# Query and key transposes one unit earlier, and the first causal mask ahead of the first expert piece, in a kernel that weaves attention into two mixtures of experts

## Chip, cores and metric

The kernel runs on one core of a Trainium2 chip. The metric is the device time of one execution in microseconds, as the median of several executions. Inputs and outputs are fp32 and lie in HBM.

## What is computed

The input x has 8 sequences of 512 tokens of 128 numbers. The reference applies three residual steps: half of a mixture-of-experts layer, causal attention, and half of the same mixture again, each on a layer norm of x.

```python
x = x + 0.5 * ffn(layernorm(x))
x = x + attn(layernorm(x))
x = x + 0.5 * ffn(layernorm(x))
```

The mixture has 8 experts (128 to 512 to 128, relu between). A router picks the two best experts of each token, and their outputs are added with softmax gates. The attention has 16 heads of 8 numbers. On half of the heads the queries and keys are rotated by position, on half a linear decay with the distance is added to the scores; all are causal. The softmax divides by the sum of the exponentials.

## The kernel before, in words

**Stages.** The first mixture takes its tokens in three groups (f0, f1, f2), the second in three (g0, g1, g2). For each group tokens are routed, scattered by expert to HBM, read back per expert, run through the expert, and their results gathered and added. The attention takes (sequence, head group of four heads, step) as one unit: 8 x 4 x 3 = 96 units, numbered 0 to 95, twelve to a sequence, three to a head group. Units below 0 and above 95 hold expert work alone. Everything is woven together in one program: while attention runs for one sequence, experts of the first mixture work for later sequences and experts of the second mixture for earlier ones.

**Order.** The order of instructions on TensorE (PE), ScalarE (ACT), VectorE (DVE) and SyncE (SP) is the order in which the program is written out; no scheduler moves them. Each engine goes through its own stream in turn, and instructions on different engines wait for each other where data or buffers require it.

**A unit** is written by `surround` (L1458). It issues, in this order:

- `scores` (L1222): score matmuls of four heads into `st` (one buffer of four PSUM banks), written transposed with keys on the partitions; then two exponentials on ScalarE (L1238), each of two heads, into `ee`. Step 0 has one key tile of 512 queries, step 1 one of 384, step 2 two of 256 and 128.
- `values` (L1251) of the unit before: matmuls of `ee` with the values into `o`; after a head group's last step ScalarE copies `o` to `oT`.
- one piece of expert work (`fill`). A piece is a transposition of gathered rows (`turn`, L996, tile xbT, copied to xT), one of four matmuls of the first layer (`wide`, L1010, tile z, relu to h), or one tile of the second layer (`out`, L1034, tile y, bias added on VectorE to ysb). `m.evac` says which engine evicts turn and wide here: VectorE in attention units, but ScalarE in units 8, 9 and 10 of a sequence.
- `causal` (L1241) for the first two heads: VectorE takes the minimum of the exponentials and a mask (L1245). Its instruction becomes the *mark*; evictions of wide and out become the mark too. An indirect DMA on POOL (scatter, send, gather) is made to wait for the last mark, which keeps these transfers apart.
- `m.transfer`: one such indirect DMA.
- `outputs` (L1268) of the head group that ended: transposes, a reciprocal and a multiplication on VectorE.
- `causal` for the other two heads.
- the work due in this unit, each stream a step at a time, with expert pieces spread between (the rest of the unit's quota, some two pieces a unit in all); then additions and a second transfer.

**Due work.** `at(u, stream, steps)` (L1431) files the steps of a stream under units u, u+1 and so on; streams filed first are taken first within a unit. For sequence b with first unit u = 12 b:

- `project` (L1157) in the eight units from u - 10 to u - 3: layer norm, transposition, the matmuls for queries, keys and values (L1169), rotation (L1186 to L1192), and as the last step VectorE writes the scaled queries into `qpad` (L1195) and the keys into `kpad` (L1198). There is one qpad and one kpad; each head has 32 columns in them.
- `operands` (L1201) for head group g, two steps: four TensorE transposes of qpad (L1208) and a VectorE copy to `qT` (L1214), then the same for kpad with a ScalarE copy to `kT`. qT and kT have two buffers each.
- `finish` (output projection of the attention) and `route` (router of the second mixture; its steps on VectorE L838 to L937).

During attention three PSUM banks serve all else (pool m: pieces, transposes, projections, router), one serves `o` and four serve `st`.

Of the kernel before, what the change touches and what calls it, by code (L numbers as in the profile page):

```python
# [1333 lines left out]
def macaron_kernel(  # L1334
# [24 lines left out]
    def run(*streams):  # L1359
        for s in streams:  # L1360
            for _ in s:
                pass
# [12 lines left out]
    def take(stream, n):  # L1375

        for _ in range(n):
            if next(stream, STOP) is STOP:
                return
            yield  # L1380
# [5 lines left out]
    with ExitStack() as main:  # L1386
        m = Main(tc, main, aps)
# [17 lines left out]
        def close(g):  # L1405
            m.close_group(g, order.index(g))

        def opened(g):

            pieces = m.experts(g)  # L1410
            next(pieces)
            return pieces

        def step(*streams):
            for st in streams:
                next(st, None)

        def transfers(n):
            for _ in range(n):
                m.transfer()  # L1420
# [4 lines left out]
        units = [(b, g, s) for b in range(B) for g in range(G) for s in range(len(m.STEPS))]  # L1425
        per = len(m.STEPS)
# [4 lines left out]
        def at(u, stream, steps, each=1):  # L1431

            for k in range(steps):
                due.setdefault(u + k // each, []).append((stream, 1))

        def routed(u, shares, urgent=False, ahead=False):
            early = u < 0 or u > core
            r = m.route(shares, urgent, ahead, early)
            steps = 7 if early else 8
            if u > core:  # L1440
                at(u, r, 3 + steps, 3)
                return
            if shares[0][0] is not f1:
                at(u, r, 3)
                u += 3
            at(u, r, steps)

        def combined(u, g, i, dst=None, urgent=False, ahead=False):
            at(u, m.combine(g, i, dst, urgent, ahead), 1)
# [8 lines left out]
        def surround(n, att):  # L1458

            m.unit = n  # L1460
            now = None
            for g, fetch, start, end in plan:
                if n == fetch:
                    close(g)
                    fills[g.key] = [opened(g), g.pieces]
                if n == end:
                    run(fills[g.key][0])
                if start <= n < end:
                    now, until = fills[g.key], end
                    if g is g1 and att:  # L1470
                        until = end + 7
            quota = min(now[1], -(-now[1] // (until - n))) if now else 0
            fill = now[0] if now else iter(())
            if now:
                now[1] -= quota
            if att:
                ee = m.scores(*units[n])
            last, m.oT = m.oT, None
            if m.held is not None:
                got = m.values(*m.held)  # L1480
                if got is not None:
                    m.oT = (*m.held[:2], got)
            m.held = (*units[n], ee) if att else None
            m.evac = "dve" if att and n % seq not in (8, 9, 10) else "act"
            run(take(fill, 1 if quota else 0))
            m.evac = "act"
            if att:
                m.causal(units[n][2], ee, 0)
            m.transfer()
            if last is not None:  # L1490
                m.outputs(*last)
            if att:
                m.causal(units[n][2], ee, 1)
            if not att:
                m.additions()
            work = due.pop(n, [])
            todo = max(quota - 1, 0)
            for k, (stream, steps) in enumerate(work):
                some = todo // (len(work) - k + 1)
                run(take(stream, steps))  # L1500
                run(take(fill, some))
                todo -= some
            if n >= core and len(m.jobs) + len(m.results) > 2:
                run(take(fill, todo // 2))
                todo -= todo // 2
                m.transfer(second=True)
            run(take(fill, todo))
            m.additions()
            m.transfer(second=True)

        m.held = m.oT = None
        with m.banks(("m", 8)):

            n = [m.normalise(b) for b in range(5)]
            r = [m.route([(f0, 0)], early=True), m.route([(f0, 1)], early=True),
                 m.route([(f1, 0)], True, early=True)]
            step(n[0], n[0], n[1], n[1], n[0], n[0])
            step(r[0], n[1], n[1], r[0], r[1], r[0], r[0])
            transfers(8)
            step(r[1], r[1], r[1], n[2], n[2])  # L1520
            transfers(8)
            step(n[3], n[3], n[4], n[4], *[r[0], r[1]] * 3, n[2], n[2])
            step(r[2], r[2], r[2], n[3], n[4], n[3], n[4])
            run(*r[:2], *n)
            m.bias_columns()

            at(first, r[2], 4)
            routed(first + 1, [(f1, 1)], urgent=True)
            routed(first + 3, [(f1, 2)], urgent=True)
            routed(-22, [(f2, 0)], urgent=True)  # L1530
            combined(-16, f0, 0, urgent=True, ahead=True)
            routed(-14, [(f2, 1)], urgent=True)
            combined(-12, f0, 1, urgent=True)
            routed(-10, [(f2, 2)], urgent=True)
            at(-10, m.project(0), 8)
            for b in range(B):
                u = b * seq
                if b == 2:
                    combined(7, f1, 0, urgent=True, ahead=True)
                elif b > 2:  # L1540
                    combined(u - (17 if b == 5 else 21), *place[True][b][0], urgent=b == 5, ahead=b == 5)
                if b > 0:
                    at(u - 10, m.project(b), 8)
                for g in range(G):
                    at(u + g * per - 2, m.operands(b, g), 2)
                at(u + seq + 2, m.finish(b), 2, 2 if b == B - 1 else 1)
                routed(u + seq + (3 if b == B - 1 else 4), place[False][b], urgent=b in (1, 4, 5, 6, 7), ahead=b in (4, 6, 7))
            for i in range(2):
                combined(79 + 7 * i, g0, i, out)
            for i, (_, t0, t1) in enumerate(g1.shares):  # L1550
                at(tail + 2 + 3 * i, m.collect(g1, i, out), 1 + t1 - t0)
            at(tail, m.verdict(bad), 2)

            for u in range(first, 0):
                surround(u, False)
                if u == first:
                    m.attention_constants()
                for _ in range(min(2, len(m.loads))):
                    m.loads.popleft()()
        with m.banks(("st", 1), ("o", 1), ("m", 3)):  # L1560
            for u in range(core + 2):
                surround(u, u < core)
                if u >= 12 and m.later:
                    m.later.popleft()()
        with m.banks(("m", 8)):
            for u in range(core + 2, ends):
                surround(u, False)
            run(fills["g2"][0])
            assert not due, due
            assert not m.jobs and not m.adds  # L1570
            while m.results:
                m.transfer()
            last = [m.collect(g2, i, out, parts=min(2, g2.shares[i][2] - g2.shares[i][1])) for i in range(4)]
            step(*last)
            run(*last)
# [53 lines left out]
```

## Time and profile before

| | us |
|---|---|
| median of 9 runs | 695.67 (694.57 to 698.71) |
| the profiled execution | 696.78 |
| its span | 695.1 |
| TensorE matmuls busy | 623.6 |
| VectorE busy | 405.9 |
| ScalarE busy | 343.9 |
| POOL busy | 295.8 |
| first and last score matmul (start) | 145.9 and 562.0 |
| query copies to qT, 32 | 21.8 |
| key copies to kT, 32 | 18.8 |
| masks, 192 | 93.3 |

A profile is of one execution, so what is worked out from it is set against that execution's own time, 1.1 us above the median. PEld is the weight load of TensorE, which runs beside matmuls. Matmuls are pipelined and their ends are modelled, so that the start of the next one tells more than the end of the last. A line of the timeline gives start and length in us, engine, line of the kernel, operation, tiles out and in, shapes and a count; in brackets stands how long the engine sat idle before it and what ended that.

### The profile page before, as it was taken

To read this page: it belongs to the slowest core of one execution; us is meant where nothing else is said; L and a number is where in the kernel's file an instruction comes from. 1 tells how busy PE (TensorE), PEld (TensorE's weight loads), DVE (VectorE), ACT (ScalarE), POOL (GpSimd) and SP (SyncE) were. 2 spreads that over 40 slices of the span, in tenths; PEclk is the share of its full clock that TensorE was granted. 3 is DMA by queue.
4 is the path that set the end of the run, shared out by engine and by line. 5 is a ranking of instruction groups with operands and counts; after the bars stand their busy time and mean duration, and the time that the engine had idled before them with its cause. 6 is when DMAs were issued, how large, how long until landed. Compare 5 with 4: busy or idle time off the path is not lost. (4 is left out here: it accounts for less than half of the span.)

```text
span 695.1 us, 12906 instructions
## 1 busy us (share of the span) xinstructions
PE 623.6 (90%) x4797; PEld 403.5 (58%) x4797; DVE 405.9 (58%) x1432; ACT 343.9 (49%) x552; POOL 295.8 (43%) x318
## 2 busy tenths in 40 slices
PE   3269989999999999999999999989999998979980
PEld 2148867756556656555656566545556566747760
DVE  6736437735457575675676687777666654333424
ACT  4034434455665656566566566566645542234420
POOL 3745627653132314414144425333244556665550
PEclk9999999999999999999999999999999998999995
DMA  8747843222409951011211111112212121145224
GB/s 264 197 136 204 213 111 100 71 63 71 106 24 143 199 193 38 24 27 42 71 29 43 49 33 37 31 31 71 60 30 63 32 58 42 39 137 150 82 66 153
DMA packets 80229, 61.32 MB, mean 88 GB/s; under 512 B 7400, under 2 KB 73888, under 8 KB 80160
## 3 DMA queue, kind: packets, MB, share of 16 engines
q1 hardware_dynamic: 71296, 42.79, 24.2%
q0 software_dynamic: 8576, 17.63, 8.5%
q8 instruction: 40, 0.66, 0.4%
q14 instruction: 29, 0.24, 0.1%
q10 hardware_dynamic: 288, 0.01, 0.0%
HBM read 26.21 MB, written 34.19 MB: 87 GB/s over the span
## 5 line engine op out<-in xcount | busy, mean ns | idle before, releaser
L1238 ACT ACTIVATE ee<-st 128x768 f32<-128x768 f32 (+1 forms) x192 | 159.2, 882 | 90.4 <-PE st L1231 85.1
L479 POOL DMA_INDIRECT yt_f<-ys,back_f x64 | 65.3, 1020 | 130.8 <-DVE ee L1245 55.9
L1245 DVE TENSOR_TENSOR ee<-ee,keep 128x256 f32<-128x256 f32 (+1 forms) x192 | 93.3, 507 | 22.2 <-ACT ee L1238 21.9
L1037 PEld LDWEIGHTS y_f<-w_sb,h_f 128*120 128x120 f32 (+1 forms) x704 | 85.9, 182 | 28.5 <-issue 16.2
L1231 PE MATMUL st<-qT,kT 32*128 32x512 f32 (+3 forms) x1024 | 96.1, 467 | 5.7 <-ACT kT L1214 3.3
L1037 PEld LDWEIGHTS y_g<-w_sb,h_g 128*128 128x128 f32 x640 | 81.3, 193 | 32.2 <-issue 25.5
L895 POOL DMA_INDIRECT xs<-xn_g,to_g x64 | 63.9, 999 | 84.7 <-DVE ee L1245 32.5
L1037 PE MATMUL y_f<-w_sb,h_f 128*120 128x128 f32 (+1 forms) x704 | 93.9, 277 | 0.2 <-DVE h_f L1022 0.2
L1013 PE MATMUL z_f<-xT_f,w_sb 128*128 128x480 f32 (+1 forms) x192 | 90.8, 562 | 1.0 <-ACT xT_f L1004 1.0
L1013 PE MATMUL z_g<-xT_g,w_sb 128*128 128x512 f32 (+1 forms) x192 | 89.7, 554 | 1.4 <-ACT xT_g L1004 0.7
L1257 PE MATMUL o<-ee,vpad 128*32 128x512 f32 (+3 forms) x1024 | 89.6, 442 | 0.8 <-DVE ee L1245 0.8
L1020 ACT ACTIVATE h_f<-z_f,b1T 128x480 f32<-128x480 f32 (+1 forms) x86 | 53.6, 625 | 70.1 <-PE z_f L1013 69.4
L1037 PE MATMUL y_g<-w_sb,h_g 128*128 128x128 f32 x640 | 85.9, 279 | 0.5 <-DVE o_tok L1280 0.3
L981 POOL DMA_INDIRECT ys<-ysb_g,home_g x64 | 62.9, 983 | 51.2 <-ACT h_g L1020 16.7
L1020 ACT ACTIVATE h_g<-z_g,b1T 128x512 f32<-128x512 f32 (+1 forms) x77 | 49.5, 645 | 54.1 <-PE z_g L1013 53.8
L1041 DVE TENSOR_TENSOR ysb_f<-y_f,b_sb 120x128 f32<-120x128 f32 (+1 forms) x88 | 25.1, 288 | 79.4 <-PE y_f L1037 75.7
L1041 DVE TENSOR_TENSOR ysb_g<-y_g,b_sb 128x128 f32<-128x128 f32 x80 | 23.2, 291 | 77.6 <-PE y_g L1037 73.7
L1231 PEld LDWEIGHTS st<-qT,kT 32*128 32x128 f32 x1024 | 43.1, 183 | 39.0 <-ACT kT L1214 11.4
L895 POOL DMA_INDIRECT xs<-xn_n,to_f x40 | 39.0, 975 | 35.7 <-ACT xi_sb L732 8.8
L1257 PEld LDWEIGHTS o<-ee,vpad 128*32 128x32 f32 x1024 | 23.7, 108 | 52.5 <-issue 5.5
L1013 PEld LDWEIGHTS z_g<-xT_g,w_sb 128*128 128x128 f32 x192 | 29.9, 194 | 21.3 <-issue 12.8
L1013 PEld LDWEIGHTS z_f<-xT_f,w_sb 128*128 128x128 f32 x192 | 30.9, 197 | 14.6 <-issue 8.1
(185 smaller groups left out, 771.0 us busy)
## 6 DMA issues: line engine op xcount, KB each, us to landing
xs<-zeros SPq DMA_DIRECT2D x8, 520.0 KB
xb_g<-xs SPq DMA_DIRECT2D x16, 260.0 KB
w_sb<-in_L_ffn_W_dram SPq DMA_DIRECT2D x16, 256.0 KB
xb_f<-xs SPq DMA_DIRECT2D x16, 240.0 KB
ys<-ysb_f SPq DMA_DIRECT2D x16, 240.0 KB
ys<-zeros SPq DMA_DIRECT2D x2, 1664.0 KB
x<-in_L_attn_x_dram SPq DMA_DIRECT2D x8, 256.0 KB
xs<-zeros SPq DMA_DIRECT2D x1, 1920.0 KB
```

Source lines behind the costliest of these rows:

```text
L479: ins = op(*args, **kw)
L895: ins = nc.gpsimd.indirect_dma_start(out=g.xs[:, :], out_offset=bass.IndirectOffsetOnAxis(ap=to[:, t, r : r + 1], axis=0), in_=xn[:, t, : ...
L981: ins = nc.gpsimd.indirect_dma_start(out=g.ys[:, :], out_offset=bass.IndirectOffsetOnAxis(ap=home[e][:rows, t : t + 1], axis=0), in_=ys[:r ...
L1013: nc.tensor.matmul(z[:, :n], self.w1_sb[:, e, ts(c, P)], xT[:, n0 : n0 + n], start=True, stop=True,)
L1020: ins = nc.scalar.activation(dst, z[:, :n], AF.Relu, bias=bias)
L1037: nc.tensor.matmul(y[:rows], h[:, c, ts(t, rows)], self.w2_sb[:, e, c, :], start=(c == 0), stop=(c == C - 1),)
L1041: ins = nc.vector.tensor_tensor(ys[:rows, t, :], y[:rows], self.b2_sb[:rows, e], ALU.add)
L1231: nc.tensor.matmul(st[:, h, c0 : c0 + N - kt * P], kT[r0 : r0 + SLOT, ts(kt, P)], qT[r0 : r0 + SLOT, kt * P :], start=True, stop=True,)
L1238: nc.scalar.activation(ee[:, two, :width], st[:, two, :width], AF.Exp)
L1245: ins = self.nc.vector.tensor_tensor(d, d, self.keep.unsqueeze(1).unsqueeze(1).to_broadcast([P, 2, len(parts), P]), ALU.min,)
L1257: self.nc.tensor.matmul(self.o[h * SLOT : (h + 1) * SLOT, kt * P :], self.vpads[b % 2][:, kt, 4 * g + h, :], ee[:, h, c0 : c0 + n], start= ...
```

## The change

Two edits. The first files the two steps of `operands` one unit earlier: queries in unit u + 3 g - 3 and keys in u + 3 g - 2, where they were in u + 3 g - 2 and u + 3 g - 1 (u the sequence's first unit, g the head group). For group 0 the query step now falls into unit u - 3, that of the last step of `project`, behind it. The second moves the call of `causal` for the first two heads ahead of the unit's first expert piece, so that on VectorE the mask stands before the eviction of that piece. The instructions are the same ones.

```diff
             m.evac = "dve" if att and n % seq not in (8, 9, 10) else "act"
+            if att:
+                m.causal(units[n][2], ee, 0)
             run(take(fill, 1 if quota else 0))
             m.evac = "act"
-            if att:
-                m.causal(units[n][2], ee, 0)
             m.transfer()
...
                 for g in range(G):
-                    at(u + g * per - 2, m.operands(b, g), 2)
+                    at(u + g * per - 3, m.operands(b, g), 2)
```

## The prediction

> **What bounds the kernel now.** I read the page first, then the stretch of the attention units, then what TensorE waits for, and last one unit in order of time.
>
> ```profile
> PE 623.6 (90%) x4797; PEld 403.5 (58%) x4797; DVE 405.9 (58%) x1432; ACT 343.9 (49%) x552; POOL 295.8 (43%) x318
> ## 2 busy tenths in 40 slices
> PE   3269989999999999999999999989999998979980
> ```
>
> TensorE is busy in 90% of the span, and its idle time lies at the two ends. The 96 attention units run from 145.85 (first score matmul) to 564.13. The windows view (length, then PE, PEld, DVE, ACT and POOL busy with instructions, granted clock, DMA share, GB/s) has for them:
>
> ```profile
> 145.85:564.13 418.28, 411.10 (x3530) 243.10 (x3531) 269.88 (x859) 250.73 (x396) 146.09 (x143) 1.00 0.26 62
> ```
>
> TensorE idles 7.2 us of 418, at the full clock; VectorE is busy 65%, ScalarE 60%. So a unit (4.36 us on average) lasts as long as TensorE's own work, and whatever makes TensorE wait there is added to the time nearly whole. What it waits for in this stretch (us, times, longest):
>
> ```profile
> PE st L1231 <- ACT kT L1214: 3.3, 8, 0.7
> PE st L1231 <- ACT ee L1238: 1.5, 3, 0.6
> PE qkv_ps_a L1169 <- DVE o_tok L1280: 1.4, 4, 0.7
> ```
>
> This is all that an earlier transpose or mask can win: score matmuls that wait for the copy of the keys or for the exponentials, and little else.
>
> **Transposes one unit sooner.** No instruction is added or removed: 32 times four query and four key transposes (0.6 us a group), 32 VectorE copies of 0.68 us and 32 ScalarE copies of 0.59 us move by one unit. They issue no DMA, and SP's and POOL's orders stay. What changes is where each stands in the in-order streams of TensorE, VectorE and ScalarE.
>
> The gain: the key copy, now in the unit just before its scores, goes a unit ahead, so the 3.3 us go. The weight-load row for the same wait says 11.4 us (17 times); but a load of st also idles 0.70 where nothing holds it ("issue", at 307.79), so I stay near the lower end: -4.0, bounds -3.3 and -11.4. What is late next is the score bank, which frees when the exponentials end, about 2.5 us after the scores start in the units with two of 0.8 us; those units stay longer than that. The 1.5 us of waits for exponentials (0.21 at 355.86, 0.64 at 452.95, the third of 0.6 too) all stand after a unit with the widest scores, which now gets 0.6 us of query transposes: -1.4.
>
> The loss: for group 0 of a sequence, the query transposes now stand in the very unit in which VectorE writes the padded queries (qpad, L1195), the last step of project. Until now a unit lay between. In TensorE's new order of that unit (the last group's unit 0) come scores, values, one expert piece, then the query transposes, then the rest. VectorE's order there is: masks, for sequences 2 to 7 four steps of the router (L841 to L848), qpad, kpad, the query copy. Sequence 3, TensorE first, then VectorE:
>
> ```profile
> 299.96 1.14 PE L1231 MATMUL st<-qT,kT 32*128 32x512 f32 x8
> 301.03 0.86 PE L1257 MATMUL o<-ee,vpad 128*32 128x256 f32 x16
> 301.82 0.63 PE L1000 MATMUL xbT_ps_f<-ident,xb_f 120*128 120x120 f32 x4
> 302.29 0.98 PE L1013 MATMUL z_f<-xT_f,w_sb 128*128 128x480 f32 x2
> 303.19 0.93 PE L1231 MATMUL st<-qT,kT 32*128 32x384 f32 x8
> ```
>
> ```profile
> 303.14 0.47 DVE L1245 TENSOR_TENSOR ee<-ee,keep 128x256 f32<-128x256 f32 x1 [0.25 <-ACT ee L1238]
> 303.54 0.41 DVE L841 TENSOR_TENSOR eq_g<-eq_g,before 128x256 f32<-128x256 f32 x1
> 303.99 0.42 DVE L844 TENSOR_TENSOR gt_g<-gt_g,eq_g 128x256 f32<-128x256 f32 x1
> 304.44 0.42 DVE L846 TENSOR_REDUCE rank_g<-gt_g 128x32 f32<-128x256 f32 x1
> 304.90 0.18 DVE L848 TENSOR_SCALAR mask_g<-rank_g 128x32 bf16<-128x32 f32 x1
> 304.99 0.42 DVE L1195 TENSOR_SCALAR qpad<-qkv_a 128x512 f32<-128x512 f32 x1
> ```
>
> TensorE would reach the transposes after the first piece (xbT), at 302.29; qpad is written at 305.41. It waits 3.1 us, and behind the waiting transpose stand z, which could have run, and the next unit's scores, for which ScalarE waits. VectorE cannot be sooner: its second mask waits for the second exponential, which follows from the same unit's scores, and four more instructions stand between it and qpad. The same reading (start of what follows the first piece, end of qpad): sequence 1, 192.67 to 194.06, 1.4 (no router steps); 2, 246.95 to 249.59, 2.6; 4, 355.08 to 358.06, 3.0 (of four z passes I take half, less the 0.21 wait); 5, 405.10 to 408.10, 3.0; 6, 452.17 to 455.32, 3.2 (z passes as long as at sequence 4); 7, 502.02 to 504.60, 2.6. Together 18.9. From qpad's end to the first transpose it took 0.1 us at 139.8: seven times, +0.7. At sequence 5 the mask no longer stands behind y's eviction: -0.3. Sum +19.3; bounds 15 (VectorE half a microsecond sooner each time) and 23.
>
> Sequence 0 has its projection before the attention, where TensorE is the bound too (100.7 of 105 us from 40 to 145). It would come to the transposes at 136.65 and go on at 139.85, 3.2 us; 0.9 of such a wait is there already (query transposes for qpad, once). +2.2, bounds 0 and 3.2.
>
> **The mask in front.** In 9 of 12 units the first piece is evicted by VectorE. Moving the first mask (0.42 or 0.69 us) ahead of that eviction makes the eviction wait for the first exponential, and queued behind it are the second mask and all of VectorE's later work. But that exponential ends about 2.2 us after the scores start (299.96 to 302.20), and the first piece, behind scores and values, ends about 2.3 to 2.9 after; so the mask falls into time in which VectorE stood idle, and the second mask is sooner by up to one mask. Masks held TensorE once, for 0.8 us. Best: all its waits for VectorE in the stretch, 0.8 + 1.4 + 0.3 + 0.2 + 0.2 = -2.9. Worst: the single eviction that waited longest behind exponentials, +3.5. I take 0, as nearly all is hidden behind TensorE's own work; if that cover is gone, the PSUM bank of the first piece comes free late and the third next matmul waits. The mark behind which POOL's transfers stand becomes that eviction, on ScalarE in units 8 to 10. The tokens' additions come two units (8.7 us) after a gather of 1 us; 0.
>
> **The clock.** A wait also costs afterwards. Around the wait of TensorE for the first rows of a group of experts:
>
> ```profile
> 90.97:94.38 3.41, 1.54 (x14) 1.21 (x13) 1.68 (x9) 0.56 (x1) 0.00 (x0) 1.00 0.80 215
> 94.38:97.80 3.42, 3.42 (x8) 1.72 (x7) 0.49 (x4) 1.22 (x2) 0.00 (x0) 0.50 0.74 168
> ```
>
> Busy 1.54 of 3.41 us, in waits of 1.3 and 0.6, and the next 3.41 us ran at half the granted clock: 1.7 us lost. 582.50 to 585.90 (busy 1.77) and 609.80 to 613.20 (0.93) were followed by half clock too; 606.40 to 609.80 (1.48) was not. Seven of the eight waits above are 2.6 to 3.2 us. If about 1.9 idle of 3.41 is what it takes, a wait of 3 us in a random place leaves that in some 7 of 10 cases: 5 x 1.6 = +8.0, bounds 0 and 7 x 1.7 = 12.
> The Trainium skill, "TensorE: Matmul & The Clock Gate", Part 1, says that the clock halves only after at least one idle window of about 3.4 us; none of these waits is that long, so by the page this term would be 0 and the sum 8 us lower. The trace shows half clock after waits of 1.3 and 0.6 us, and the trace decides.
>
> **The sum.** +19.3 + 2.2 - 4.0 - 1.4 + 0 + 8.0 = +24.1 us. The profiled execution took 696.78 us (span 695.1 and 1.7 around it), which gives 720.9; the median of the nine runs is 1.1 below, 695.67, so I forecast 719.8.
>
> **Rivals.** (1) The waits without the clock: +16.1, 711.8. For it: no half clock in all of the attention stretch, though TensorE waits up to 0.8 us there; a wait that a window boundary splits leaves only 1.5 in each. Against: three slow stretches after waits of this size. (2) On the other side: qpad is written before TensorE comes to it. Then only the gains count, -5.4, 690.3. Its place is the last group's unit 0, and it decides as soon as the eight waits add up to less than 5.4 us, 0.7 each. For it: today TensorE waits for qpad only once, 0.9. Against: today a unit lies between, and qpad still ends 0.5 to 2.5 us into the next unit. (3) Waits near the low bound and the gain near 11.4: 15 + 0 - 11.4 - 1.4 - 2.9 is about 0, 695.
>
> **The numbers.** Forecast (waits and some clock, 713 to 729) 0.62; rival 1 (706 to 713) 0.27; rival 2 0.05; rival 3 and what lies within 0.2% (about what a measurement of this kernel can tell from no change) 0.03; slower outside the range 0.03. Faster by over 0.2%: 0.05, within: 0.03, slower: 0.92. The range: rival 1 with waits of 15 instead of 19.3 and the mask's -2.9 is +8.9 (705); the forecast with waits of 23 and a clock term of 12 is +31.8 (728). 705 to 728.
>
> **What will show it.** Right: the row of query transposes waiting for qpad goes from 0.9 us, once, to some 22 us, eight times; keys and scores leave the list; the attention stretch grows from 418.3 to about 436 to 441; granted clock of 0.50 after some of the waits. Wrong: if VectorE's router steps come after qpad, or TensorE runs z ahead of the waiting transposes, the eight waits vanish; if the clock stays at 1.00, rival 1 holds.

## The result, and the profile after

| | before, us | after, us |
|---|---|---|
| median (range, runs) | 695.72 (693.59 to 698.95, 31) | 719.90 (716.27 to 724.70, 10) |
| ratio after / before, 95% interval | | 1.0344 (1.0323 to 1.0366) |
| the profiled execution | 696.78 | 722.63 |
| its span | 695.1 | 720.9 |
| TensorE matmuls busy | 623.6 | 634.8 |
| mean granted clock of TensorE | 0.978 | 0.958 |

The changed kernel is 24.2 us slower, 0.1 us from the forecast. The first part of the page of after, with the slices of TensorE and of its clock:

```profile
PE 634.8 (88%) x4797; PEld 408.9 (57%) x4797; DVE 414.5 (57%) x1432; ACT 346.1 (48%) x552; POOL 294.8 (41%) x318
## 2 busy tenths in 40 slices
PE   3269999899999899989989989979989998979980
...
PEclk9999999999999999989989989989999999889995
```

Before, the middle of TensorE's row was nearly all 9. Now an 8 or a 7 stands about every third slice (a sequence is some three slices of 18 us) from the fourteenth on, and under four of these there is an 8 in the clock's row too. And the same 4797 matmuls keep TensorE busy 11.2 us longer: that is not waiting, that is a slower clock. The attention stretch, the same 3530 matmuls as in the line of before (length, then busy time of each engine, clock, DMA share, GB/s):

```profile
147.46:589.62 442.16, 422.06 (x3530) 247.86 (x3531) 278.53 (x860) 252.95 (x396) 145.40 (x143) 0.97 0.24 59
```

It grew from 418.28 to 442.16. TensorE idles 20.1 us in it instead of 7.2, and is busy 422.1 instead of 411.1. What TensorE waits for (us, times, longest):

```profile
PE qT_ps L1208 <- DVE qpad L1195: 22.5, 8, 3.7
...
PE qkv_ps_a L1169 <- DVE o_tok L1280: 0.4, 1, 0.4
PE o L1257 <- DVE ee L1245: 0.3, 1, 0.3
PE st L1231 <- ACT ee L1238: 0.2, 1, 0.2
```

The wait for qpad leads the list, eight times, where it had been 0.9 once. The row of scores waiting for the key copy (3.3) is gone from the whole answer; the exponentials went from 1.5 to 0.2, `o_tok` from 1.4 to 0.4.

The unit in front of sequence 3 (the one whose order the prediction wrote out) in TensorE's timeline of after, then in VectorE's:

```profile
306.56 1.14 PE L1231 MATMUL st<-qT,kT 32*128 32x512 f32 x8
307.63 0.86 PE L1257 MATMUL o<-ee,vpad 128*32 128x256 f32 x16
308.42 0.63 PE L1000 MATMUL xbT_ps_f<-ident,xb_f 120*128 120x120 f32 x4
312.16 1.09 PE L1208 MATMUL qT_ps<-ident,qpad 128*128 128x128 f32 x4 [3.11 <-DVE qpad L1195]
313.04 1.01 PE L1013 MATMUL z_f<-xT_f,w_sb 128*128 128x480 f32 x1
```

```profile
309.46 0.75 DVE L1245 TENSOR_TENSOR ee<-ee,keep 128x256 f32<-128x256 f32 x2
310.13 0.42 DVE L841 TENSOR_TENSOR eq_g<-eq_g,before 128x256 f32<-128x256 f32 x1
310.59 0.42 DVE L844 TENSOR_TENSOR gt_g<-gt_g,eq_g 128x256 f32<-128x256 f32 x1
311.05 0.42 DVE L846 TENSOR_REDUCE rank_g<-gt_g 128x32 f32<-128x256 f32 x1
311.50 0.18 DVE L848 TENSOR_SCALAR mask_g<-rank_g 128x32 bf16<-128x32 f32 x1
311.59 0.42 DVE L1195 TENSOR_SCALAR qpad<-qkv_a 128x512 f32<-128x512 f32 x1
```

Both masks, four router steps, then qpad without a pause; TensorE stands 3.11 us in front of the transposes, with z behind them ready. The transposes that then run take 1.09 us instead of 0.63: the clock is halved at that moment. The windows view around it says so:

```profile
308.16:311.57 3.41, 0.89 (x16) 0.46 (x8) 3.27 (x11) 2.49 (x4) 1.22 (x1) 1.00 0.01 2
311.57:314.98 3.41, 2.82 (x10) 1.45 (x14) 1.47 (x4) 0.10 (x1) 0.00 (x0) 0.50 0.09 24
314.98:318.40 3.42, 3.42 (x17) 0.68 (x18) 0.42 (x1) 2.08 (x3) 0.00 (x0) 0.50 0.00 0
318.40:321.80 3.40, 3.40 (x34) 2.66 (x34) 1.79 (x6) 1.23 (x2) 0.94 (x1) 1.00 0.03 6
```

TensorE was busy 0.89 us of the first window; the next two are at 0.50, the fourth is back at 1.00.

### The profile page after: what moved, and what is told of

Same layout as the page of the kernel before. It is cut to its first block, busy times and chain, and to the rows that moved or that the text cites. A ratio compares the mean times of both kernels' runs of the same rounds, so it can differ in the third digit from the quotient of the medians.

```text
span 720.9 us, 12897 instructions
## 1 busy us (share of the span) xinstructions
PE 634.8 (88%) x4797; PEld 408.9 (57%) x4797; DVE 414.5 (57%) x1432; ACT 346.1 (48%) x552; POOL 294.8 (41%) x318
## 5 line engine op out<-in xcount | busy, mean ns | idle before, releaser
L1245 DVE TENSOR_TENSOR ee<-ee,keep 128x256 f32<-128x256 f32 (+1 forms) x192 | 98.0, 511 | 103.0 <-ACT ee L1238 102.4
L1231 PE MATMUL st<-qT,kT 32*128 32x512 f32 (+3 forms) x1024 | 99.8, 482 | 1.0 <-ACT h_f L1020 0.8
L1257 PE MATMUL o<-ee,vpad 128*32 128x256 f32 (+3 forms) x1024 | 93.4, 457 | 0.3 <-DVE ee L1245 0.3
L1013 PE MATMUL z_g<-xT_g,w_sb 128*128 128x512 f32 (+1 forms) x192 | 92.2, 567 | 1.4 <-DVE e_g L933 0.7
L1208 PE MATMUL qT_ps<-ident,qpad 128*128 128x128 f32 x128 | 21.4, 293 | 22.5 <-DVE qpad L1195 22.5
```

What stands on the lines that cost most here:

```text
L1013: nc.tensor.matmul(z[:, :n], self.w1_sb[:, e, ts(c, P)], xT[:, n0 : n0 + n], start=True, stop=True,)
L1208: self.nc.tensor.transpose(tp[:, ts(t, P)], pad[:, t, 4 * g : 4 * g + 4, :].rearrange("p h s -> p (h s)"), self.ident,)
L1231: nc.tensor.matmul(st[:, h, c0 : c0 + N - kt * P], kT[r0 : r0 + SLOT, ts(kt, P)], qT[r0 : r0 + SLOT, kt * P :], start=True, stop=True,)
L1245: ins = self.nc.vector.tensor_tensor(d, d, self.keep.unsqueeze(1).unsqueeze(1).to_broadcast([P, 2, len(parts), P]), ALU.min,)
L1257: self.nc.tensor.matmul(self.o[h * SLOT : (h + 1) * SLOT, kt * P :], self.vpads[b % 2][:, kt, 4 * g + h, :], ee[:, h, c0 : c0 + n], start= ...
```

## The experiments

Three sets of four kernels; each set ran on a chip of its own, with runs of the kernel before beside it: 709.25 us (median of 23), 696.89 (11) and 708.1 (11). So ratios, and differences inside one set, are what is compared. The first and the third chip are called the slower ones. Where a unit is called longer or shorter, its length is taken from one start of score matmuls to the next and set against the first profile of before, the one shown ahead of the prediction.

### First set: each half alone, and the groups apart

**mask_only.** Only the mask moves in front.

```diff
+            if att:
+                m.causal(units[n][2], ee, 0)
             run(take(fill, 1 if quota else 0))
             m.evac = "act"
-            if att:
-                m.causal(units[n][2], ee, 0)
```

> The mask in front alone; the transposes stay where they were. My theory (the mask falls into time in which VectorE stood idle, and TensorE hardly waits for VectorE): 695.7, within 1.0 either way; idle time of VectorE before the masks, waiting for ScalarE, goes from 22 to about 100 us as in the changed kernel, and TensorE's waits stay as they were. Rival (the mask edit carries part of the loss, since the eviction queued behind the mask holds a PSUM bank): over 699, with waits of TensorE for ScalarE or VectorE in front of the expert pieces.

Measured: 713.53 us, ratio 1.0060 (1.0035 to 1.0085). Small, but not nothing: the expectation (no change) missed, and the rival's sign is there. TensorE waits in front of expert pieces for evictions: 4.5 us for VectorE's `h_g` and `h_f`, in five waits, and 1.3 for ScalarE's `h_f`. In before there are two such waits, of 0.2 each. How that comes about is shown after the third set.

**transposes_only.** Only the transposes move.

```diff
-                    at(u + g * per - 2, m.operands(b, g), 2)
+                    at(u + g * per - 3, m.operands(b, g), 2)
```

> The transposes one unit sooner alone; the first mask stays behind the first piece's eviction. My theory: the whole loss is here, 719 to 722, TensorE waits for qpad 22 to 23 us, eight times. Rival (the mask edit matters): below 717.

Measured: 736.51 us, 1.0382 (1.0343 to 1.0421). TensorE waits for qpad 21.7 us, seven times; the eighth wait, 1.4 us, the view puts down to ScalarE's `h_f`. This edit alone brings the loss.

**group0_only.** Of the transposes only those of group 0 move, and no mask.

```diff
-                    at(u + g * per - 2, m.operands(b, g), 2)
+                    at(u + g * per - (2 if g else 3), m.operands(b, g), 2)
```

> Only head group 0 of each sequence has its transposes one unit sooner; groups 1 to 3 and the mask stay. My theory: the loss of the changed kernel without most of its gain: 722 to 726, waits for qpad 22 us, and the waits of the scores for the key copies go down by no more than a third. Rival (moving all groups costs, by the banks or by VectorE's load): about a quarter of the loss, 702.

Measured: 738.41 us, 1.0419 (1.0362 to 1.0476); the wait for qpad 23.4 us, eight times. The waits for keys stay (3.7, eight times).

**groups123.** The complement, with the mask: groups 1 to 3 move, group 0 stays.

```diff
-                    at(u + g * per - 2, m.operands(b, g), 2)
+                    at(u + g * per - (3 if g else 2), m.operands(b, g), 2)
```

> Both edits, but head group 0 keeps its transposes where they were, one unit behind the write of qpad; only groups 1 to 3 move. My theory: the eight waits and their half clock are gone and the gain is left: 689 to 693 (4.0 less for the keys, of which a group 0 keeps a quarter or so, and 1.4 for the exponentials); waits for qpad at most 0.9 us as before. Rival (the gain was never there, the scores then wait for the exponentials instead): 695 to 696.

Measured: 706.49 us, 0.9972 (0.9942 to 1.0001). The wait for qpad is 0.8, once. So all of the loss is group 0's, as the prediction had it; the gain of the others is 0.28%, where 0.38% was the least that was expected (693 us), and its interval just takes in no change. On this chip the waits for keys fell to 1.4, but those for exponentials rose to 3.4.

### Second set: is the clock a term of its own?

**changed_again** is the changed kernel, on the same chip as the three after it.

> The changed kernel itself, beside the two that follow and on the same chip: 1.034 times the kernel before, eight waits for qpad of 22 to 23 us.

Measured: 721.92 us, 1.0368 (1.0333 to 1.0403), with eight waits for qpad, 22.5 us in all.

**warm_waits.** The changed kernel with 16 useless transposes of the identity, into the bank that the query transposes then overwrite, ahead of group 0's query transposes. TensorE gets more work and does it where it would wait.

```diff
+            if g == 0 and name == "qT":
+                for k in range(16):
+                    self.nc.tensor.transpose(tp[:, ts(k % T, P)], self.ident, self.ident)
```

> The changed kernel with more work: sixteen transposes of the identity (about 0.1 us each, 1.7 us in all) stand ahead of the query transposes of head group 0 and fill part of the wait for qpad; their result is overwritten. The end of each wait stays where it is. My theory (the waits cost a second time, by the half clock that follows them): faster than the changed kernel by 6 to 11 us though it does 13 us more of TensorE work, no 0.50 clock during attention. Rival (the clock has no part, the waits are all): the same time as the changed kernel, within 1 us, or up to 1 us slower for the one wait that is shorter than the fill.

Measured: 710.48 us, 1.0198 (1.0164 to 1.0231): 11.4 us faster than changed_again, a little above what was expected, with 128 matmuls more. Its wait row, and its clock:

```profile
PE qT_ps L1211 <- DVE qpad L1195: 8.6, 7, 2.0
```

```profile
PEclk9999999999999999999999999999999999889995
```

qpad is no sooner; the waits are only filled. One half-clock window is left in the attention units, after the longest wait (sequence 6); the slices are too coarse to show it, the trace has it at 466.4. TensorE's busy time is 636.4 us beside 634.0 in changed_again, though 128 matmuls came on top. This can't be had from waits alone, so the rival "waits without the clock" falls and the clock is worth about 11 us.

**qpad_first.** The changed kernel, with project's last step first among the work due in its unit, ahead of the router steps.

```diff
-        def at(u, stream, steps, each=1):
+        def at(u, stream, steps, each=1, front=False):
...
-                due.setdefault(u + k // each, []).append((stream, 1))
+                work = due.setdefault(u + k // each, [])
+                work.insert(0 if front and k == steps - 1 else len(work), (stream, 1))
...
-                    at(u - 10, m.project(b), 8)
+                    at(u - 10, m.project(b), 8, front=True)
```

> The changed kernel with the last step of the projection (writes of qpad and kpad) ahead of the router's four steps in their unit, instead of behind them. My theory: each wait of sequences 2 to 7 is shorter by the 1.45 us of those four steps, so 22.5 goes to about 14, and waits of 1.3 to 1.8 us rarely bring the half clock: 14 to 18 us faster than the changed kernel, 1.009 to 1.014 times the kernel before. Rival (VectorE's order there does not matter, it is the write's own time behind the second mask): less than 4 us faster.

Measured: 702.27 us, 1.0080 (1.0056 to 1.0103): 19.7 us faster than changed_again, above the range expected. The wait row:

```profile
PE qT_ps L1208 <- DVE qpad L1195: 11.8, 7, 3.0
```

The eighth wait (sequence 4, 1.5 us) the view puts down to ScalarE's `h_g`; with it the waits are 13.4 us, 9.1 less. TensorE's busy time is 9.1 us less too (624.9 beside 634.0): the clock now halves twice before and in the attention units (at 139 and 460) instead of five times. The four router steps between the masks and qpad were some half of each wait of sequences 2 to 7 (1.5 to 1.7 us of 2.6 to 3.7).

**control** is the kernel before, profiled on this chip.

> The kernel before, for a profile on this chip: no wait for qpad over 0.9 us. If this chip is the slower one, its exponentials start late in some units here too, without a wait of TensorE behind them; my theory of the mask needs that. Rival: TensorE waits there in the kernel before as well, so that the mask in front has no part.

Measured: 694.61 us, span 692.9; every attention unit as long as in the first profile of before, within 0.1 us, and the longest wait for qpad 0.9. But this is the faster chip, so what was asked of it, whether late exponentials on a slower chip cost the kernel before anything, stays without an answer.

### Third set: the gain, without the wait

**groups123_plain.** Groups 1 to 3 move, the mask stays.

```diff
-                    at(u + g * per - 2, m.operands(b, g), 2)
+                    at(u + g * per - (3 if g else 2), m.operands(b, g), 2)
```

> The kernel before with only the transposes of head groups 1 to 3 one unit sooner; the first mask stays behind the first piece's eviction. My theory (the waits of the scores for keys and exponentials, 4.8 us, mostly go; no new wait for qpad): 0.990 to 0.995 times the kernel before, and on a chip whose exponentials start late in some units faster than the same with the mask in front (there 0.997). Rival (the gain is taken by other waits): 0.998 to 1.002.

Measured: 705.67 us, 0.9976 (0.9949 to 1.0002). As with the mask in front (0.9972 on the first chip), and short of the 0.990 to 0.995 expected: waits for keys fell to 1.1 us, those for exponentials rose to 3.0.

**qpad_sooner.** The changed kernel with project's last step taken one unit earlier too (the seventh and the eighth step share a unit), so that a unit lies between qpad and its transposes again.

```diff
-                    at(u - 10, m.project(b), 8)
+                    p = m.project(b)
+                    at(u - 10, p, 7)
+                    at(u - 4, p, 1)
```

(and the same for sequence 0)

> The changed kernel with the projection's last step (writes of qpad and kpad) one unit sooner too, in the unit of the rotation, so that a unit lies again between the write and the transposes of group 0. My theory: the long waits are gone. From the trace of before the rotation ends 0.4 us and more ahead of where TensorE comes to the transposes, but for sequences 4 and 6 (0.2 and 0.6 late) and 0 (1.7 late): 2 to 3 us of waits for qpad left, 0.992 to 0.997 times the kernel before. Rival (an earlier write is no cure, for VectorE is loaded as much there and the masks come late): over 1.003.

Measured: 702.31 us, 0.9925 (0.9900 to 0.9951): faster than both kernels. Its wait rows:

```profile
PE qT_ps L1208 <- DVE qpad L1195: 3.8, 4, 1.7
...
PE st L1231 <- ACT ee L1238: 2.6, 4, 0.9
```

No half clock in the attention units, no row for keys. From the start of the first unit to that of the last it takes 412.45 us, in the first profile of before 415.51. These 3.1 us are about half of the 5.8 between the medians; where the rest lies isn't shown, as there is no profile of before on this chip.

**qpad_sooner_plain.** The same with the mask where it was.

> The same as qpad_sooner, but with the first mask behind the first piece's eviction as in the kernel before. My theory of the mask (worth nothing where exponentials are on time, a loss where they are late): within 0.15% of qpad_sooner on the faster chip, 0.3 to 0.8% faster than it on the slower one. Rival (the mask in front is of use once VectorE is loaded more): slower than qpad_sooner by 0.2% or more.

Measured: 706.95 us, 0.9987 (0.9963 to 1.0010). So in this company the mask in front is worth 0.6%, though alone it costs: the expectation had the opposite sign for a slower chip, and its rival came true. The two profiled executions are 7.4 us apart (699.63 and 707.00), but 3.5 us of that lie ahead of the first attention unit, where both programs are the same (that of qpad_sooner_plain has half clock from 94.2 to 101.0), and about 2.5 follow a half-clock window after the wait of sequence 6. Why the medians differ is not settled.

**mask_only_again.** The edit of mask_only, on this chip.

> The mask in front alone, a second time. If this is the faster chip: 0.999 to 1.001 times the kernel before. If it is the slower one: 1.004 to 1.008 again.

Measured: 708.43 us, 1.0024 (0.9997 to 1.0050). Less than on the first chip and than the 1.004 to 1.008 expected of a slower one, and not clearly above 1.

**What the mask does there** can be read in mask_only's timeline, sequence 3's last unit (lines left out between):

```profile
364.73 0.94 PE L1231 MATMUL st<-qT,kT 32*128 32x256 f32 x16
...
366.37 0.70 PE L1013 MATMUL z_g<-xT_g,w_sb 128*128 128x256 f32 x2
...
367.50 1.51 ACT L1238 ACTIVATE ee<-st 128x768 f32<-128x768 f32 x2 [3.95 <-PE pos_ps_g L869]
368.34 0.69 DVE L1245 TENSOR_TENSOR ee<-ee,keep 128x512 f32<-128x512 f32 x1 [2.20 <-ACT ee L1238]
...
368.95 0.48 DVE L1022 TENSOR_SCALAR h_g<-z_g,b1T 128x256 f32<-128x256 f32 x1
...
369.49 0.44 PE L1000 MATMUL xbT_ps_g<-ident,xb_g 128*128 128x128 f32 x2 [1.81 <-DVE h_g L1022]
```

The exponentials start 2.8 us after the scores; in the same unit of before it is 1.0 (360.11 to 361.11). The mask waits for them, the eviction of z waits behind the mask although z is long done, z's PSUM bank is held, and TensorE waits 1.81 us for it. mask_only is longer by 0.6 us in unit 11, 0.9 in 29, 1.5 in 47 and 1.5 in 53. All its attention units together are 4.3 us longer than in the first profile of before, which is from another chip, and 4.3 us is also what lies between the medians. All eight profiles of the first and third sets start exponentials 0.5 to 1.8 us late in units 11, 29, 53 and 74 and in some others. The two profiles of before have no such unit, nor have those of the second set and after, but for some of 0.5 to 0.7 us inside half-clock stretches; all of these are from faster chips. What makes ScalarE late there stays open: the view names the router's `pos_ps_g`, which the exponentials don't read. With the mask behind, late exponentials cost less, but not nothing. group0_only leaves the order around unit 53 as it was: the exponentials are 1.6 late there as in mask_only, and the unit is 0.45 longer instead of 1.5; in unit 74 they are 1.2 late and it is 0.85 longer. With the transposes moved as well the order of the mask makes no such difference in unit 53 (0.15 longer in groups123, 0.1 in groups123_plain).

## Why the prediction was right, point by point

**The waits for qpad.** Right: each to about 0.4 us, while the sum agrees to the tenth only because the errors cancel. Idle time in brackets of after's eight rows, beside what the prediction read from VectorE's order (its gap and the 0.1):

| sequence | 0 | 1 | 2 | 3 | 4 | 5 | 6 | 7 | sum |
|---|---|---|---|---|---|---|---|---|---|
| predicted | 3.2 | 1.5 | 2.7 | 3.2 | 3.1 | 2.8 | 3.3 | 2.7 | 22.5 |
| measured | 2.98 | 1.16 | 2.87 | 3.11 | 3.08 | 3.00 | 3.71 | 2.57 | 22.5 |

transposes_only and group0_only have the loss without the mask and without the other groups, groups123 has neither the wait nor the loss. The wait is what group 0 brought, and no z ran ahead of the waiting transposes.

**Keys and exponentials.** Right: keys -3.3 (predicted -4.0; the weight-load row's 11.4 was not the size), exponentials -1.3 (-1.4). A row not counted on, `o_tok`, gave -1.0. On chips where exponentials start late this gain is smaller (groups123: keys to 1.4, exponentials up to 3.4), and the transposes of groups 1 to 3 alone are not clear of no change there (0.9972 and 0.9976).

**The mask in front.** Taken at 0 with +3.5 as the worst. On the chip of after it costs nothing that can be seen in any unit, although VectorE now does wait for exponentials (no run there has the mask edit alone):

```profile
L1245 DVE TENSOR_TENSOR ee<-ee,keep 128x256 f32<-128x256 f32 (+1 forms) x192 | 98.0, 511 | 103.0 <-ACT ee L1238 102.4
```

Its idle time ahead of masks is 103.0 us, 22.2 before: the cover that the prediction named holds this. TensorE's one wait for a mask went from 0.8 to 0.3; the prediction counted that 0.8 to the stretch, but it lies behind it, at 565.5. Where exponentials start late the cover is gone, and what follows is the chain that the prediction wrote down for that case (bank late, a later matmul waits): +0.2% to +0.6% for the mask alone. With transposes and qpad moved the mask in front came out 0.6% better instead, so no single price of this edit on the slower chips is shown.

**The clock.** The mechanism was right, and the count came out too (five), though which five was left to chance. The size was too small: 8.0 predicted; TensorE's busy time grew 11.2 us (11.0 of it in the attention stretch), and warm_waits took 11.4 away. The mis-sized term is the 1.6 us for each: it was 2.2 on average, because four of the five half-clock times lasted two windows of 3.41 us, not one. The trace of before had this already behind 585.90 (columns as above, clock third from the end):

```profile
585.90:592.70 6.80, 6.02 (x21) 4.42 (x22) 3.98 (x14) 1.26 (x2) 3.13 (x4) 0.50 0.11 39
```

The last section says what tells the two lengths apart.
The Trainium skill, "TensorE: Matmul & The Clock Gate", Part 1, says that the clock halves after an idle window of about 3.4 us, and that these windows run freely. The 3.413 us grid of the trace agrees with the second. On the first, windows that held 0.78 to 1.26 us of work were enough here, in waits from 2.87 us on, so an idle window need not be empty, and read as the prediction read it the rule is wrong by the whole term.

**The sum.** Waits +21.6, keys -3.3, exponentials -1.3, `o_tok` -1.0, clock +11.2 make +27.2; the profiled executions are 25.9 apart and the medians 24.2. So the sum came out as close as it did partly by luck: the clock was 3 us too small, the measured terms add up to 1.3 us more than the two executions are apart (where they overlap isn't shown), and the profiled execution of after happens to lie 2.7 us above its median, that of before 1.1.

**The rivals.** Rival 1 (711.8) is what warm_waits comes near: 1.0198 of 695.67 is 709.4, the time of the kernel whose clock is nearly kept up. As a forecast it failed, since the clock did drop. Rival 2 (690.3, -0.8%) is what qpad_sooner comes near, at 0.9925, with 3.8 us of waits for qpad left. That the transposes alone bring this gain isn't shown: with the mask behind, the same order of transposes and qpad gave 0.9987. Rival 3 falls with the keys at 3.3.

## What to carry to other kernels

Before a step is moved up in an in-order stream, look where its input is written on the other engine in that same unit: the start of the next matmul and the end of that write, read from the trace of before, gave eight waits to within half a microsecond. If the producer can move as well, move both; that turned +3.4% into -0.75% (on another chip, and with both edits; without the mask in front it gave no clear gain). And count what a wait costs afterwards: here half as much again as the waits themselves, as the clock drops.

## What the runs showed of the hardware

**When the clock halves.** The trace records the granted clock in windows of 3.413 us. Laid on that grid, over the fourteen profiles of this case (from 70 us into the span to 15 us before the last matmul), a full-clock window in which TensorE was busy at most 1.4 us was followed by half clock 38 times of 38; between 1.4 and 1.8 us, 10 of 30; between 1.8 and 2.7 us, 8 of 129, all of them after 584 us, outside the attention units. So the eight waits of after sort themselves by how the grid cuts them: windows with 0.78, 0.89, 1.26, 0.97 and 1.03 us of work (sequences 2 to 6) were followed by half clock, 1.54 and 1.62 (0 and 7) and 2.25 (1) were not. A wait of 3 us cut in the middle by a window's edge can cost only itself: the wait of sequence 0 left 2.31 and 1.54 us of work in its two windows, and the clock stayed. In changed_again, the same kernel with the same waits to 0.02 us, the grid lies elsewhere: there the 2.98 us of sequence 0 left 1.29 us in one window and brought half clock, while the 2.86 of sequence 2, cut into windows of 1.67 and 2.30, did not.

**When it comes back.** If TensorE was busy for the whole first half-clock window, the clock was back after it in 26 cases of 28; if not, it stayed low for at least one more in 27 of 28. In after the wait reached into that window four times (2.82 of 3.41 busy at 311.57, for one), and those four are the longer ones.

**Filling a wait is worth work.** 128 useless transposes made the changed kernel 11.4 us faster (710.48 against 721.92), though it stays 2% above the kernel before.

**One program, several chips.** The kernel before took 695.7, 709.3, 696.9 and 708.1 us on the chips of this case, 2% apart; every kernel profiled on the slower ones has late exponentials at the same units, though before itself was not profiled there. A difference of half a per cent is read within one chip only, and an edit can be worth different things on two of them (mask_only 1.0060 and 1.0024).
